# A fused convolution-attention and feed-forward kernel: x loaded one pair later, weight sums one step later, half a layer norm earlier

## The chip, the cores and the metric

The kernel runs on one core of one Trainium2 chip. A core has five engines that work beside each other and meet at semaphores: TensorE (PE in the profile; its weight loads are PEld), VectorE (DVE), ScalarE (ACT), GpSimd (POOL), and SyncE (SP), which here only issues transfers. Transfers are issued from the SP, ACT and POOL queues and are carried by the core's 16 DMA engines. The metric is the device time of one execution in microseconds, as the median of several runs.

## The reference, cut to what matters

Eight images of 32 x 32 positions with 384 channels go through two layers. The first is an attention over all 1024 positions with six heads and relative position terms; the second is a causal attention with one head of 384, and, for the images whose quantization group exists, a feed-forward part with sign weights. There are five groups of one image each, so images 0 to 4 have the feed-forward part and images 5 to 7 don't (their rows of it are zero).

```python
# layer 0
x = x + attention_6_heads(group_norm(x), rel_pos_h, rel_pos_w)  # softmax(q k + rel_h + rel_w) v, then proj
# layer 1
t = tokens(x)
t = t + causal_attention(layer_norm(t), Wq, Wk, Wv)             # softmax(mask(q k / sqrt(384))) v
n = layer_norm(t)                                               # "the second norm" below
h = gelu(quantize(n @ sign(W1 - mean_group(W1)).T + b1))
t = t + quantize(h @ sign(W2 - mean_group(W2)).T + b2)
```

`mean_group` is a mean over a fifth of the output features of the weight matrix; `quantize` scales an image to 8 bits by its largest absolute value.

## The kernel before

Images are worked on one after the other. In layer 0 the six heads are three pairs; a pair's scores come in six bursts (`BURSTS`, 16 units of one block of keys and one half of the queries), and the value products of a burst follow behind the scores of the next. Each unit's exponentials are written into a page of a ring of 12 pages of [128, 1024], and VectorE adds them up (`sums`), which frees the page. The relative position terms of a pair are made in pages of the same ring (`far0`, `far1`, `near`), written to DRAM and read back in another order, split by `place` into a high and a low part, and brought to their places (`r`) by 16 transfers, half of them issued by SP and half by GpSimd.

```python
            def place(p, near, pages):
                for d in range(2):
                    hi, lo, src = (...)
                    nc.scalar.copy(hi, src)                                              # L497
                    nc.vector.tensor_tensor(lo, src, hi.bitcast(F32), ALU.subtract)      # L498
                    if d == 0:
                        yield
                for part in range(4):
                    for d in range(2):
                        for i in range(2):
                            half = part % 2 if d else part // 2
                            (nc.gpsimd if i else nc.sync).dma_start(out=r[part]...,      # L505
                                                                    in_=pages[i]...)
...
            def residual():
                xt = load_x(pools, b)                        # four transfers of 384 KB, issued by SP
                for j in range(NJ):
                    nc.gpsimd.tensor_tensor(xt[:, j, :], xt[:, j, :], pb, ALU.add)       # L551
                return xt
```

The loop over pairs and bursts:

```python
            for p in range(NPAIR):
                sums = [...]
                for n, burst in enumerate(bursts):
                    prs = [scores(p, *u) for u in burst]              # PE L568, L572; ACT L578
                    if b == 0 and (p, n) == (0, 1):
                        multiply_out(pools)                           # wqk: PE L286, evicted by DVE L287
                    for u in pending:
                        values(*u)                                    # DVE L586 (sums), PE L589
                    if n == 0:
                        if p > 0:
                            few = set_aside(p - 1, *last)             # ACT L608, DVE L612, L613
                        elif b > 0:
                            xt = residual()
                        avs = [...]
                    if b == 0 and xt is None and next(signs[0]):
                        xt = residual()
                    if p == 0:
                        with tc.issue_after(last_exp[0]):
                            next(later, None)                         # place() of pairs 1 and 2
                    if n == 2 and p > 0:
                        divide(p - 1, few)                            # PE L621, DVE L597 to L625
                    pending = [...]
```

In image 0 a generator runs beside this: it loads W1 and W2 in three pieces, sums them by group (`w` pieces), forms the means, loads them again (`sign` pieces), makes signs and stores them in DRAM.

```python
        for which, w, _, n_out, _ in pieces("w"):            # the load is issued in pieces()
            for g in range(NG):
                nc.vector.tensor_reduce(part[...], w[:, :, ts(g, n_out // NG)], AX.XY, ALU.add)   # L234
            times[which] += 1
            if which == 1 or w.shape[1] > 1:
                yield False
        ...                                                  # all-reduce of the sums, means
        for which, w, dst, n_out, last in pieces("sign"):
            ...                                              # above = w > m; w = sign (L256, L257)
                    if done > 600:
                        done = 0
                        yield False
            ...
            if last:
                yield True
```

Layer 1's attention goes over eight blocks of keys, its value products two blocks behind, and the feed-forward part begins with the second norm, in two halves of four row blocks each:

```python
            for c in range(NJ):
                prs.append(scores(c))                        # PE L793, DVE L798, ACT L800
                next(other, None)
                for work in signs:
                    next(work, None)
                if c >= 2:
                    values(c - 2)                            # PE L806, DVE L807 to L809
            ...
            values(NJ - 2)
            values(NJ - 1)
...
        def ffn(xt, b, gn):
            xs = [...]
            for half in range(2):
                rs = layer_norm_T(xt, xs[0], half, f"2_{b}", xs[1])
                if half == 0 and gn is not None and pools.fast:
                    with tc.issue_after(last_transpose[0]):
                        ahead[b + 1, 0] = project_qk(b + 1, gn, 0)            # PE L422
```

`layer_norm_T` takes the statistics of four row blocks (DVE L343, L344), a root (ACT L347), and then for each block writes the normalized rows to `xn`, a pool of three buffers (DVE L360), transposes them (PE L298), copies the result rounded (ACT L353) and subtracts to get the rest (DVE L354).

Of the kernel before, what the change touches and what calls it, by code (L numbers as in the profile page):

```python
# [73 lines left out]
def conv_attn_hybrid(  # L74
# [142 lines left out]
    def binarize(pools):  # L217

        def pieces(name):
            for n, piece in enumerate(PIECES):
                room, at = pools.flat(f"{name}_{n}"), 0
                for i, (which, src, sign, k0, k1, n_out) in enumerate(piece):
                    w = room[:, at : at + (k1 - k0) * n_out].rearrange("p (k o) -> p k o", o=n_out)
                    at += (k1 - k0) * n_out
                    nc.gpsimd.dma_start(out=w, in_=src.rearrange("(k p) o -> p k o", p=P)[:, k0:k1, :])
                    yield which, w, sign[:, k0 * n_out : k1 * n_out], n_out, i + 1 == len(piece)

        part = const.tile([P, 2, 2, NG], F32, name="sums_w")  # L230
        times = [0, 0]
        for which, w, _, n_out, _ in pieces("w"):
            for g in range(NG):
                nc.vector.tensor_reduce(  # L234
                    part[:, times[which], which, g : g + 1], w[:, :, ts(g, n_out // NG)], AX.XY, ALU.add
# [53 lines left out]
    def stages(pools):  # L289
# [266 lines left out]
        def attend0_fast(residual, b, q, k, r, v, later):  # L556
# [91 lines left out]
            for p in range(NPAIR):  # L648
                sums = [pools.page(f"sum0_{b}_{p}_{half}") for half in range(2)]
                for n, burst in enumerate(bursts):  # L650
# [5 lines left out]
                    if n == 0:  # L656
                        if p > 0:
                            few = set_aside(p - 1, *last)
                        elif b > 0:
                            xt = residual()  # L660
                        avs = [pools.o_tile(f"av0_{b}_{p}_{half}") for half in range(2)]
                    if b == 0 and xt is None and next(signs[0]):
                        xt = residual()
                    if p == 0:
                        with tc.issue_after(last_exp[0]):
# [73 lines left out]
            return xt, lambda j: None  # L739


        def attention1(xt, more, b, between):
            xT, q = pools.halves(f"lnT_1_{b}"), pools.halves(f"q1_{b}")
            v = pools.flat(f"v1_{b}").rearrange("p (j c) -> p j c", j=NJ)
            nc.gpsimd.memset(v[:, :, C:], 1.0)
# [28 lines left out]

            room = between()
            got = next(room, None)
            (attend1_fast if pools.fast else attend1_general)(xt, b, q, xT, v, room)
            return got

        def attend1_fast(xt, b, q, xT, v, other):  # L780

            room = [pools.flat(f"pr1_{b}_{i}") for i in range(2)]
            tot = pools.small.tile([P, NJ], F32, tag="tot1", name=f"tot1_{b}")
# [30 lines left out]
            for c in range(NJ):  # L814
                prs.append(scores(c))
                next(other, None)
                for work in signs:
                    next(work, None)
                if c >= 2:
                    values(c - 2)  # L820
            for work in signs:
                assert next(work, None) is None
            signs.clear()
            values(NJ - 2)
            values(NJ - 1)
            check(tot, rt, b * (NPAIR + 1) + NPAIR)

        def attend1_general(xt, b, q, xT, v, other):
            next(other, None)
            mask = pools.work.tile([P, P], F32, tag="mask", name=f"mask_{b}")  # L830
            make_causal_mask(nc, mask, mask_val=MASKED)
# [52 lines left out]
            return w1k, w2m  # L884

        def ffn(xt, b, gn):
            xs = [pools.halves(f"{n}_{b}", F32R) for n in ("lnT_2", "lnlo_2")]
            for half in range(2):
                rs = layer_norm_T(xt, xs[0], half, f"2_{b}", xs[1])

                if half == 0 and gn is not None and pools.fast:
                    with tc.issue_after(last_transpose[0]):
                        ahead[b + 1, 0] = project_qk(b + 1, gn, 0)
# [68 lines left out]
                for j in range(NJ):  # L962
                    nc.vector.scalar_tensor_tensor(xt[:, j, :], y[:, j, :], s, xt[:, j, :], ALU.mult, ALU.add)

            return add

        signs = []
        unfinished = []
# [1 line left out]
        def run(pools):  # L970
# [7 lines left out]
            for b in range(B):  # L978
# [4 lines left out]
                    if b + 1 < B:  # L983
                        yield from group_norm_T(b + 1)

                gn = attention1(xt, more, b, between)
                add = ffn(xt, b, gn) if b < B_FFN else None

                def finish(b=b, xt=xt, add=add):
                    if add:  # L990
# [59 lines left out]
```

## Time and profile before

| what | before |
|---|---|
| median of 3 runs | 2481.92 us (2478.55 to 2483.06) |
| span of the profiled execution | 2479.7 us |
| image 0 to 4, one each (layer 0, layer 1, feed-forward) | about 331 us |
| image 5 to 7, one each (no feed-forward) | about 260 us |
| VectorE busy | 1418.0 us (57%) |
| ScalarE busy | 1032.1 us (42%) |
| GpSimd busy | 287.1 us (12%) |
| TensorE's granted clock, mean of the run | 0.99 |

A line of the timeline reads: start and length in us (of a merged group of equal instructions), engine, line of the kernel, operation, output and input tiles, shape, count; in brackets the idle time of the engine ahead of it and the instruction that ended it. A line of the waits reads: engine and its waiting operation, the releaser, and then the total in us, the number of times and the longest. All line numbers are those of the kernel before.

### The profile page before, as it was taken

What the parts mean: (1) busy time and instruction counts of PE and PEld (TensorE: products, weight loads), DVE (VectorE), ACT (ScalarE), POOL (GpSimd) and SP (SyncE); (2) the same over time, 40 slices, a digit from 0 to 9 for tenths busy, and PEclk for the clock granted to TensorE, in tenths of its full rate; (3) what the DMA queues carried; (4) which work ended last, traced back from release to release, by engine and by line L of the source; (5) the groups of instructions that cost most, each with busy time, mean ns of one, the idle gap of its engine ahead of it and who ended that gap; (6) DMA issues with size and microseconds to landing.
All of it is one profiled execution on the core that took longest, in us unless ns stands there. A gap on an engine that the chain in (4) does not pass through costs nothing.

```text
span 2479.7 us, 25709 instructions
## 1 busy us (share of the span) xinstructions
PE 2407.4 (97%) x9378; PEld 1285.8 (52%) x9378; DVE 1418.0 (57%) x2182; ACT 1032.1 (42%) x1756; POOL 287.1 (12%) x389
## 2 busy tenths in 40 slices
PE   7899999999999999999999999999999999999998
PEld 3335585345764456743558534567445443554344
DVE  4596554963466744657545487346674357524752
ACT  3351373532555423645127353256542245124520
POOL 1220002300014000040000230001400030003100
PEclk9899999999999999999999999999999999999999
DMA  7622207211055101181110721004500260018000
GB/s 163 217 77 102 77 1 167 62 64 38 1 102 128 52 13 39 26 184 46 39 39 1 160 70 64 17 22 91 139 26 0 79 149 28 0 47 161 22 1 27
DMA packets 154792, 169.97 MB, mean 69 GB/s; under 512 B 113408, under 2 KB 126048, under 8 KB 153120
## 3 DMA queue, kind: packets, MB, share of 16 engines
q1 hardware_dynamic: 134416, 98.93, 16.9%
q0 software_dynamic: 17184, 69.22, 9.4%
q8 instruction: 77, 1.26, 0.2%
q10 hardware_dynamic: 3056, 0.08, 0.1%
q14 instruction: 59, 0.48, 0.1%
HBM read 75.38 MB, written 42.47 MB: 48 GB/s over the span
## 4 chain that ended last, share of the span: by engine, by line
PE 89%; POOL 4%; DVE 2%; DMA 2%; issue 1%; ACT 1%; SPq 0%; ACTq 0%; DVEq 0%; POOLq 0%
PE f_s L568 12%; PE f_av L589 11%; PE f_qk L422 10%; PE f_s L793 8%; PE f_av L806 8%; PE f_y L949 7%; PE f_y L908 7%; PE f_v L370 5%; PE f_v L517 5%; PE f_q L750 5%; POOL f_x L551 3%; PE f_s L572 3%; PE f_pj L370 2%; PE f_rel L467 2%; PE f_pj L680 2%
## 5 line engine op out<-in xcount | busy, mean ns | idle before, releaser
L578 ACT ACTIVATE f_pr<-f_s 128x512 f32<-128x512 f32 x768 | 408.1, 598 | 377.7 <-PE f_s L572 296.6
L568 PE MATMUL f_s<-f_q,f_k 64*128 64x512 f32 x1536 | 422.4, 616 | 20.3 <-DVE wqk L287 11.0
L589 PE MATMUL f_av<-f_pr,f_v 128*64 128x512 f32 x1536 | 368.7, 608 | 16.3 <-ACT f_pr L578 16.3
L586 DVE TENSOR_TENSOR f_sum<-f_sum,f_pr 128x1024 f32<-128x1024 f32 x288 | 368.3, 1329 | 17.2 <-ACT f_pr L578 16.9
L572 PE MATMUL f_s<-f_r,unit 64*128 64x512 f32 x768 | 312.2, 777 | 0.0
L422 PE MATMUL f_qk<-f_gnT,wqkv_sb 128*128 128x512 f32 x576 | 262.1, 609 | 1.6 <-DVE f_gnT L333 1.6
L568 PEld LDWEIGHTS f_s<-f_q,f_k 64*128 64x128 f32 x1536 | 148.4, 188 | 195.8 <-issue 106.7
L589 PEld LDWEIGHTS f_av<-f_pr,f_v 128*64 128x64 f32 x1536 | 99.6, 137 | 241.5 <-issue 196.4
L793 PE MATMUL f_s<-f_q,f_lnT 128*128 128x512 f32 (+3 forms) x576 | 195.9, 488 | 0.0
L806 PE MATMUL f_av<-f_v,f_pr 128*128 128x385 f32 x576 | 194.5, 486 | 0.0
L422 PEld LDWEIGHTS f_qk<-f_gnT,wqkv_sb 128*128 128x128 f32 x576 | 109.4, 194 | 144.9 <-issue 136.2
L800 ACT ACTIVATE f_pr<-f_s 128x512 f32<-128x512 f32 (+3 forms) x96 | 47.1, 491 | 262.3 <-DVE f_s L798 213.6
L806 PEld LDWEIGHTS f_av<-f_v,f_pr 128*128 128x128 f32 x576 | 108.6, 190 | 78.6 <-issue 11.5
L505 POOL DMA_DIRECT2D f_r<-f_far x192 | 102.2, 534 | 390.4 <-DVE f_far L498 348.1
L793 PEld LDWEIGHTS f_s<-f_q,f_lnT 128*128 128x128 f32 x576 | 102.0, 190 | 77.8 <-issue 54.0
L912 ACT ACTIVATE f_h<-f_y,b_sb 128x256 f32<-128x256 f32 x240 | 100.9, 472 | 68.4 <-PE f_y L908 68.4
L572 PEld LDWEIGHTS f_s<-f_r,unit 64*128 64x128 f32 x768 | 80.8, 189 | 90.9 <-issue 89.0
L750 PE MATMUL f_q<-f_lnT,wqk 128*128 128x512 f32 x288 | 127.5, 592 | 0.0
L919 DVE TENSOR_REDUCE am<-f_h 128x1 f32<-128x1024 f32 (+2 forms) x80 | 71.5, 946 | 97.3 <-ACT f_h L912 97.3
L370 PE MATMUL f_v<-wv_sb,f_lnT 128*128 128x384 f32 x384 | 126.5, 486 | 0.0
L517 PE MATMUL f_v<-wqkv_sb,f_gnT 128*128 128x384 f32 x384 | 125.2, 486 | 0.0
L551 POOL TENSOR_TENSOR f_x<-f_x,pb 128x384 f32<-128x384 f32 x64 | 107.2, 1705 | 18.4 <-DMA f_x<-in_x 18.1
(162 smaller groups left out, 2997.7 us busy)
## 6 DMA issues: line engine op xcount, KB each, us to landing
f_far<-f_far SPq DMA_DIRECT2D x48, 512.0 KB, 3.4
f_r<-f_far POOLq DMA_DIRECT2D x192, 128.0 KB, 3.0
f_r<-f_far SPq DMA_DIRECT2D x192, 128.0 KB, 2.8
f_gnT<-in_xT SPq DMA_DIRECT2D x24, 512.0 KB, 4.6
f_x<-in_x SPq DMA_DIRECT2D x32, 384.0 KB, 6.1
out_y<-f_x POOLq DMA_DIRECT2D x28, 384.0 KB, 4.4
f_near<-f_far SPq DMA_DIRECT2D x128, 64.0 KB, 4.3
f_w1a<-w1s POOLq DMA_DIRECT2D x5, 1536.0 KB, 6.8
```

Source lines behind the costliest of these rows:

```text
L370: nc.tensor.matmul(ps[:, :C], xT[:, k, ts(j, P)], w[:, k, cols], start=(k == 0), stop=(k == NC - 1))
L422: nc.tensor.matmul(made[half], wqkv_sb[:, i, ts(m, P)], xT[:, i, ts(half, 512)], start=(i == 0), stop=(i == NC - 1))
L517: nc.tensor.matmul(ps, keys[:, i, j // 2, j % 2], wqkv_sb[:, i, 2 * C :], start=(i == 0), stop=(i == NC - 1))
L551: nc.gpsimd.tensor_tensor(xt[:, j, :], xt[:, j, :], pb, ALU.add)
L568: nc.tensor.matmul(sc[par], k[rows[par], p, ts(c, P)], q[rows[par], p, ts(half, 512)], start=True, stop=False)
L572: nc.tensor.matmul(sc[par], unit[rows[par], c // 2 % 2].rearrange("i h w -> i (h w)"), r[2 * (c // 4) + c % 2][rows[par], p, ts(half, 512) ...
L578: last_exp[0] = nc.scalar.activation(pr[:, ts(par, 512)], sc[par], AF.Exp).ins
L586: nc.vector.tensor_tensor(sums[half], prev, pr, ALU.add)
L589: nc.tensor.matmul(avs[half][ts(par, HD), :], v[:, c, ts(h, HD)], pr[:, ts(par, 512)], start=(c == 0), stop=(c == NJ - 1),)
L750: nc.tensor.matmul(ps, wqk[:, k, ts(m, P)], xT[:, half, k, :], start=(k == 0), stop=(k == NC - 1))
L793: nc.tensor.matmul(sc[:, lo:], xT[:, c // 4, k, ts(c % 4, P)], q[:, half, k, lo:], start=(k == 0), stop=(k == NC - 1),)
L806: nc.tensor.matmul(av[:, : C + 1], prs[c][:, ts(j - c, P)], v[:, c, :], start=(c == 0), stop=(c == j))
```

## The change

Three things are moved; no operation is added or removed.

The load of x and the adds of pb to it come in the second burst of pair 1 instead of the first burst of pair 0 (images 1 to 7; in image 0 they still follow the first signs). They are only needed at the end of layer 0, and GpSimd also issues transfers of the position terms in pair 0.

The sums of a weight piece come one step of the generator after its load, so that VectorE doesn't stand waiting for the load. The generator has four steps more for it; so that it still ends within layer 1 of image 0, two steps are made there for each block of keys.

The first half of the second norm is put ahead of the last two value products of layer 1, so that PE has those products to do behind its transposes.

```diff
@@ binarize
         for which, w, _, n_out, _ in pieces("w"):
+            yield False
             for g in range(NG):
                 nc.vector.tensor_reduce(
@@ loop over pairs and bursts
                         if p > 0:
                             few = set_aside(p - 1, *last)
-                        elif b > 0:
-                            xt = residual()
                         avs = [pools.o_tile(f"av0_{b}_{p}_{half}") for half in range(2)]
-                    if b == 0 and xt is None and next(signs[0]):
+                    if b == 0 and xt is None and next(signs[0]) or b > 0 and (p, n) == (1, 1):
                         xt = residual()
@@ attend1_fast
                 next(other, None)
-                for work in signs:
+                for work in 2 * signs:
                     next(work, None)
                 if c >= 2:
                     values(c - 2)
             ...
             signs.clear()
+            start()
             values(NJ - 2)
             values(NJ - 1)
@@ ffn
                 rs = layer_norm_T(xt, xs[0], half, f"2_{b}", xs[1])
 
+                if half == 0:
+                    yield
                 if half == 0 and gn is not None and pools.fast:
@@ run
-                gn = attention1(xt, more, b, between)
-                add = ffn(xt, b, gn) if b < B_FFN else None
+                started = []
+
+                def start(gn):
+
+                    if b < B_FFN and not started:
+                        started.append(ffn(xt, b, gn))
+                        next(started[0])
+
+                gn = attention1(xt, more, b, between, start)
+                start(gn)
+                add = next(started[0]) if started else None
```

More of the change, by code (lines that the diff above doesn't have):

```diff
@@ L739, in attend0_general, with attention1 @@
             return xt, lambda j: None
-        def attention1(xt, more, b, between):
+        def attention1(xt, more, b, between, start):
             xT, q = pools.halves(f"lnT_1_{b}"), pools.halves(f"q1_{b}")
@@ L776, in attention1, with attend1_fast @@
             got = next(room, None)
-            (attend1_fast if pools.fast else attend1_general)(xt, b, q, xT, v, room)
+            (attend1_fast if pools.fast else attend1_general)(xt, b, q, xT, v, room, lambda: start(got))
             return got
-        def attend1_fast(xt, b, q, xT, v, other):
+        def attend1_fast(xt, b, q, xT, v, other, start):
             room = [pools.flat(f"pr1_{b}_{i}") for i in range(2)]
@@ L826, in attend1_fast, with attend1_general @@
             check(tot, rt, b * (NPAIR + 1) + NPAIR)
-        def attend1_general(xt, b, q, xT, v, other):
+        def attend1_general(xt, b, q, xT, v, other, start):
             next(other, None)
@@ L963, in add @@
                     nc.vector.scalar_tensor_tensor(xt[:, j, :], y[:, j, :], s, xt[:, j, :], ALU.mult, ALU.add)
-            return add
+            yield add
         signs = []
```

## The prediction

> **What bounds the kernel now.** I read the page's busy table first, then the list of waits of TensorE (PE), then the timeline around each of its waits.
>
> ```profile
> PE 2407.4 (97%) x9378; PEld 1285.8 (52%) x9378; DVE 1418.0 (57%) x2182; ACT 1032.1 (42%) x1756; POOL 287.1 (12%) x389
> ```
>
> TensorE is the bound: 2407.4 of 2479.7 us. No product is added or removed by the change, so it can win only the 72 us in which PE stands idle, and what products lose where they run slowly after a wait. The waits (engine, line, releaser: us in total, times, longest) say where:
>
> ```profile
> PE f_av L589 <- ACT f_pr L578: 16.3, 6, 2.8
> PE f_pt L298 <- DVE xn L360: 12.7, 13, 2.1
> PE f_gmean L320 <- DVE gmv L317: 11.3, 1, 11.3
> PE f_s L568 <- DVE wqk L287: 11.0, 1, 11.0
> PE f_s L568 <- ACT f_pr L578: 9.2, 16, 2.5
> ```
>
> The gmean wait is the first norm of image 0, which the change leaves alone. The other four are what its three parts aim at. First the wait of 11.0, in image 0 (start, length, engine, line; in brackets the idle time ahead and its releaser):
>
> ```profile
> 83.28 1.30 POOL L227 DMA_DIRECT2D f_w<-in_w1T  x2
> ...
> 94.07 4.35 DVE L234 TENSOR_REDUCE sums_w<-f_w 128x1 f32<-128x614 f32 x7 [9.15 <-DMA f_w<-in_w1T]
> 98.34 0.55 DVE L287 TENSOR_SCALAR wqk<-f_wqk 128x384 f32<-128x384 f32 x1
> ...
> 98.94 1.22 PE L568 MATMUL f_s<-f_q,f_k 64*128 64x512 f32 x1 [11.05 <-DVE wqk L287]
> ...
> 105.32 4.96 PE L589 MATMUL f_av<-f_pr,f_v 128*64 128x512 f32 x12
> ```
>
> VectorE (DVE) waits for the loaded weights, and behind it stand the three evictions of wqk, whose PSUM banks the next scores need. Then the wait in pair 0 of image 1, which images 1 to 5 and 7 repeat:
>
> ```profile
> 440.86 11.16 POOL L551 TENSOR_TENSOR f_x<-f_x,pb 128x384 f32<-128x384 f32 x6
> ...
> 451.96 3.18 POOL L505 DMA_DIRECT2D f_r<-f_far  x6
> ...
> 455.29 3.04 ACT L578 ACTIVATE f_pr<-f_s 128x512 f32<-128x512 f32 x6 [8.92 <-DMA f_r<-f_far]
> ...
> 455.94 1.56 PE L589 MATMUL f_av<-f_pr,f_v 128*64 128x512 f32 x4 [2.67 <-ACT f_pr L578]
> ```
>
> GpSimd (POOL) adds pb to x, and its transfers of pair 1's terms queue behind. They read pages of the ring that the exponentials write to, so ScalarE stands 8.92 us and PE 2.67. Last, the second norm (image 2; five images have it):
>
> ```profile
> 955.96 1.15 PE L298 MATMUL f_pt<-ident,xn 128*128 128x128 f32 x9
> ...
> 957.16 1.48 DVE L354 TENSOR_TENSOR f_lnlo<-f_pt,f_lnT 128x384 fp32r<-128x384 f32 x3
> 958.55 0.47 DVE L360 TENSOR_SCALAR xn<-f_x,lmv,lrs 128x384 f32<-128x384 f32 x1
> ...
> 959.17 0.52 PE L298 MATMUL f_pt<-ident,xn 128*128 128x128 f32 x3 [2.06 <-DVE xn L360]
> 959.52 7.01 PE L422 MATMUL f_qk<-f_gnT,wqkv_sb 128*128 128x512 f32 x12
> ```
>
> The statistics and three xn are made long before (from 924.9). The pool of xn has three buffers; the fourth xn waits for transposes and stands behind three subtractions on DVE. That, not the lateness of the norm, is the 2.06 us.
>
> [...] wqk's evictions wait out the 9.15 us of a load that they don't use. [...] six sums beside the adds take 10.93 us, 1.82 each, against 1.23 elsewhere; the adds run from 0.98 to 1.99 us. In image 6 one sum is held for 9.49 us while eight adds run at 0.97. [...] The granted clock is 0.50 from 95 to 106 us; and the twelve qk products after the 2.06 us wait take 6.7 to 7.0 us in images 1 to 3, about 5.2 in images 0 and 4.
>
> **Part 1, x at pair 1 (images 1 to 7).** In the built order the adds now stand behind all sixteen transfers of pairs 1 and 2 and the memset of v1, none among them. The pages of pair 1 are then free about 3 us after the last subtraction of its terms (436.3), near 442, while the stalled exponential was due at 446.4. So that wait goes. Worth per image: 2.67 idle, and four f_av in 1.56 us instead of 0.97 (half of x8 in 1.94), 0.6 us: 3.3. Six images: 20. Image 6: 2.49 idle, and f_av x12 in 4.57 instead of 2.79, 1.8, and slow scores, about 0.7: 5. Sum 25. Remaining in pair 0 are two waits of 0.45 at its start.
>
> The adds still run, some 8 x 1.9 = 15 us. Nothing but the queue holds them: the last terms (DVE L498, 454.26 now) come near 450 once the sums are not slowed, so the adds start near 454, when pair 1 starts, and slow the last three sums of pair 0 by 0.7 each. Transposes (2.36) and `few` (2.3) then end near 465; PE asks for them (L621) near 470. Image 0 now has its adds at 143 to 156, within pair 1, and PE shows no wait there. [...] I take 12% off: 22 us.
>
> **Part 2, sums a step behind (image 0).** The extra yields put the second load (f_w_1, 1536 KB) a step later, and its ten sums behind all three evictions. But in the built order the first five sums still stand ahead of the evictions. So DVE still waits for f_w_0, issued at 83.28. It took 10.8 us to land with 1536 KB of f_w_1 issued within 2.4 us beside it; a load of this size takes 7.7 where the next is issued behind it and 6.8 alone. I take 7 to 8: landing near 91, five sums at 0.65 (3.2), eviction near 94 instead of 98.34. The other two evictions follow at once (0.55 each) instead of among eight sums at 0.4, so the scores that now trickle from 98.94 to 105.3 are done in some 3 us. The next burst of scores, at 110.2 now, starts near 101 to 102: gain 9 us. Against it: f_w_1 lands near 97 and holds the softmax sums to about 99.5; and the ten signs of sign_0, loaded only after the means, stand in one block of 10 x (0.33 + 0.49) = 8 us ahead of pair 1's sums, so pages run short by perhaps a unit: 1 us. Net 8.
>
> **Part 3, second norm ahead (images 0 to 4).** The twelve transposes move ahead of thirty passes of the last value products (9.75 us). In the built order DVE has after value product 5: its three evictions, three subtractions, then the fourth xn. From PE's nine transposes to that xn it is the same chain: value product 5 ends at 946.24, subtractions from 947.45, xn near 948.9, PE resumes near 949.4. The wait of 2.06 moves; it doesn't go. The second half was covered with some 4 us to spare by the qk products; now it has the path product 7, sum, statistics, table load (1.28), root, xn: about 5 us against 5.15 of qk, and its fourth xn may cost 0.4. The three slow qk runs (1.75 each, 5.2 in all) may or may not recur after the moved gap. Net -1 to 0 us; I take 0 to -1.
>
> Sum: 22 + 8 - 1 = 29 us. 2481.9 - 29 = 2453.
>
> **Rivals.** (a) *The adds hurt at their new place.* For: VectorE has more to do in pair 1 than in pair 0 (set aside and divide, about 8 us)[...]. Against: image 0. It would cost 2 to 3 us an image: about 2470. (b) *The norm's wait vanishes*, if the fourth xn comes sooner than the queue says, and the clock stays full: 5 x 2.06 + 5.2 = 15 us more: about 2439. Against it is the position of that xn. (c) *The load lands as late as before*, since sixteen transfers of terms (128 KB each) share the DMA engines (0.90 to 1.02 busy from 84 to 95): then only the trickle is won, 4 us: 2457. (d) *Signs ahead stall image 0* in layer 1, where two steps of signs per row, some 4.5 us, meet rows of 5 us on PE: 2 to 4 us lost.
>
> **Range and chances.** (b) bounds it from below, (a) with (c) and (d) from above: 2439 to 2466 holds it 8 times in 10. Two per cent would be 49.6 us: all of the named waits but gmean (49 us), plus slow clocks, and part 3 keeps its share, so faster by over 2% has 0.02. Slower by over 2% needs a new wait of 11 us in every image: 0.01.
>
> **What would show it.** Right: the wait of f_av on f_pr falls from 16.3 to under 3, none on transfers of f_r; f_s on wqk falls from 11.0 to 5 to 7, f_pt on xn stays at 10 to 13. Wrong: a wait of f_den L621 or of exponentials on f_sum in pair 1; f_s on wqk near 0 or 11; f_pt near 2.

## The result and the profile after

The changed kernel takes 2452.5 us (median of 4 runs, 2450.6 to 2459.4) against 2482.3 us before (4 runs, 2478.6 to 2483.1): a ratio of 0.9888, 95% interval 0.9866 to 0.9910, or 30 us. The prediction was 2453. The profile below is of the run of 2459.4 us; a second profile of the same kernel, of a run of 2451.2 us, comes with the experiments and explains the difference.

The busy table of the changed kernel (engine, busy us, share of the span, instructions):

```profile
PE 2400.5 (98%) x9378; PEld 1286.1 (52%) x9378; DVE 1393.6 (57%) x2182; ACT 1032.6 (42%) x1756; POOL 275.2 (11%) x389
```

The same 9378 products, 6.9 us less busy than before: some of what was won is products that no longer run slowly. Now TensorE's waits (engine, tile and line, releaser: us in all, times, longest). The change shifts most line numbers by one.

```profile
PE f_pt L299 <- DVE xn L361: 12.4, 13, 2.0
PE f_gmean L321 <- DVE gmv L318: 11.3, 1, 11.3
PE f_s L569 <- DVE wqk L288: 10.6, 1, 10.6
PE f_s L569 <- ACT f_pr L579: 6.7, 15, 0.5
PE f_s L569 <- DVE seen L412: 4.0, 1, 4.0
```

Of the four waits that the change aims at, one is gone whole (f_av on f_pr, 16.3 us, six times) and one has lost its long case (f_s on f_pr: 9.2 to 6.7, longest 0.5). The other two stand: 11.0 has become 10.6, 12.7 has become 12.4. And there is a new one: scores that wait for VectorE to read the denominators (`seen`), 4.0 us.

Stage by stage, from the timelines of the two kernels (us; layer 0 is counted from its first score to the first query product of layer 1; layer 1 from there to the first product of the feed-forward part, which in images 0 to 4 includes the second norm):

| stage | before | after | gained |
|---|---|---|---|
| layer 0, image 0 | 144.67 | 150.67 | -6.0 |
| layer 0, images 1, 2, 3 | 124.91, 124.92, 125.01 | 121.55, 121.52, 121.58 | 3.4 each |
| layer 0, images 4, 5, 7 | 126.71, 126.50, 126.65 | 121.54, 121.52, 121.53 | 5.2, 5.0, 5.1 |
| layer 0, image 6 | 127.73 | 121.61 | 6.1 |
| layer 1 and second norm, images 0 to 4 | 89.49, 91.18, 91.18, 91.19, 89.49 | 91.11, 91.12, 91.12, 91.11, 91.12 | -3.1 in all |
| start, to the first score | 70.96 | 72.13 | -1.2 |

Images 1 to 7 give 31.6 us in layer 0, and image 0 and the second norm give part of it back. The start isn't touched by any of the three parts; over all the profiles here it lies between 70.96 and 73.80 us. (Image 0 is longer than the 331 us of images 1 to 4: 349 us before, from its first score to that of image 1.)

**Part 1, image 1.** Timeline around the end of pair 0 (start, length, engine and line; in brackets the idle time ahead and its releaser), GpSimd and VectorE:

```profile
458.68 2.10 POOL L506 DMA_DIRECT2D f_r<-f_far  x4 [6.67 <-DVE f_far L499]
...
460.84 3.87 POOL L552 TENSOR_TENSOR f_x<-f_x,pb 128x384 f32<-128x384 f32 x4
...
465.21 6.31 POOL L552 TENSOR_TENSOR f_x<-f_x,pb 128x384 f32<-128x384 f32 x4 [0.50 <-DMA f_x<-in_x]
...
469.61 2.36 DVE L613 STREAM_TRANSPOSE f_tr<-f_sum 128x1024 f32<-128x1024 f32 x2
471.90 2.30 DVE L614 TENSOR_REDUCE few<-f_tr 128x32 f32<-128x1024 f32 x2
...
478.39 0.26 PE L622 MATMUL f_den<-few,fold 128*64 128x32 f32 x4
```

The adds stand behind the last transfers of terms and end at 471.5. `few` is done at 474.2, and PE asks for it at 478.39 without a wait: 4 us to spare. The adds cost nothing here.

**Part 2, image 0.** Timeline around the first load of weights, in the changed kernel:

```profile
84.44 0.75 POOL L227 DMA_DIRECT2D f_w<-in_w1T  x1
...
95.58 3.59 DVE L235 TENSOR_REDUCE sums_w<-f_w 128x1 f32<-128x614 f32 x5 [9.46 <-DMA f_w<-in_w1T]
99.08 1.48 DVE L288 TENSOR_SCALAR wqk<-f_wqk 128x384 f32<-128x384 f32 x3
...
99.69 1.22 PE L569 MATMUL f_s<-f_q,f_k 64*128 64x512 f32 x1 [10.62 <-DVE wqk L288]
...
104.25 4.94 PE L590 MATMUL f_av<-f_pr,f_v 128*64 128x512 f32 x12
```

The load still lands 11.1 us after its issue, although the second one is now issued 4.6 us later. The three evictions follow each other, so the trickle of scores takes 4.6 us (99.69 to 104.25) instead of 6.4. That is all that is won here. The price comes in pair 1 of the same image:

```profile
135.99 0.67 DVE L257 TENSOR_SCALAR above<-f_sign,mean_w 128x307 f32<-128x307 f32 x2 [3.56 <-DMA f_sign<-in_w1T]
...
138.34 18.02 POOL L552 TENSOR_TENSOR f_x<-f_x,pb 128x384 f32<-128x384 f32 x8 [10.08 <-issue]
...
143.38 2.02 DVE L587 TENSOR_TENSOR f_sum<-f_pr,f_pr 128x1024 f32<-128x1024 f32 x1
...
145.50 2.06 ACT L579 ACTIVATE f_pr<-f_s 128x512 f32<-128x512 f32 x4 [4.64 <-DVE f_sum L587]
...
149.46 0.12 DVE L412 TENSOR_REDUCE seen<-f_den 128x1 f32<-128x32 f32 x1
...
149.73 1.19 PE L569 MATMUL f_s<-f_q,f_k 64*128 64x512 f32 x1 [3.95 <-DVE seen L412]
...
152.13 4.89 PE L590 MATMUL f_av<-f_pr,f_v 128*64 128x512 f32 x12
```

The same place in the kernel before (VectorE and GpSimd):

```profile
140.23 2.35 DVE L586 TENSOR_TENSOR f_sum<-f_pr,f_pr 128x1024 f32<-128x1024 f32 x2
142.50 1.22 DVE L586 TENSOR_TENSOR f_sum<-f_sum,f_pr 128x1024 f32<-128x1024 f32 x1
143.36 13.29 POOL L551 TENSOR_TENSOR f_x<-f_x,pb 128x384 f32<-128x384 f32 x8 [18.15 <-DMA f_x<-in_x]
...
143.96 0.13 DVE L411 TENSOR_REDUCE seen<-f_den 128x1 f32<-128x32 f32 x1
```

Before, the weights of the signs were issued at 99.28, the signs were done by 135.8, among the sums of pair 0, and three sums of pair 1 were made by 143.7. Now GpSimd issues these weights at 127.36, behind the all-reduce for the means, and the ten signs stand in one block (135.99 to 143.4) ahead of pair 1's first sums; those sums take 2.0 us each beside the adds instead of 1.2; the denominators are read after the third of them. Scores that want the PSUM bank (the buffer that the denominators are read from) wait 3.95 us, and then twelve f_av take 4.89 us instead of 2.79. From one product of denominators to the next, pair 1 takes 41.6 us; before it took 33.4. An estimate from these durations: without the adds the three sums would take 3.5 us instead of 5.9, so about 2.4 of the 3.95 us are the adds' and the rest comes from the late start behind the signs.

**Part 3, image 2.** Timeline of the moved norm:

```profile
947.58 1.15 PE L299 MATMUL f_pt<-ident,xn 128*128 128x128 f32 x9
...
950.10 0.47 DVE L361 TENSOR_SCALAR xn<-f_x,lmv,lrs 128x384 f32<-128x384 f32 x1
...
950.72 0.52 PE L299 MATMUL f_pt<-ident,xn 128*128 128x128 f32 x3 [1.99 <-DVE xn L361]
...
951.08 11.57 PE L805 MATMUL f_av<-f_v,f_pr 128*128 128x385 f32 x30
```

The wait has moved with its transposes, and the thirty passes behind it take 11.57 us. The clock granted to TensorE is 0.50 from 951.69 to 955.10 and 1.00 ahead of and behind that.

### The profile page after: what moved, and what is told of

The parts are those of the page before. It is cut to its first block, busy times and chain, and to the rows that moved or that the text cites. A ratio compares the mean times of both kernels' runs of the same rounds, so it can differ in the third digit from the quotient of the medians.

```text
span 2457.7 us, 25707 instructions
## 1 busy us (share of the span) xinstructions
PE 2400.5 (98%) x9378; PEld 1286.1 (52%) x9378; DVE 1393.6 (57%) x2182; ACT 1032.6 (42%) x1756; POOL 275.2 (11%) x389
## 4 chain that ended last, share of the span: by engine, by line
PE 95%; DVE 2%; DMA 1%; ACT 1%; issue 0%; POOL 0%; DVEq 0%; ACTq 0%
PE f_s L569 14%; PE f_av L590 14%; PE f_qk L423 10%; PE f_av L805 8%; PE f_s L792 8%; PE f_y L952 7%; PE f_y L911 7%; PE f_v L371 5%; PE f_v L518 5%; PE f_q L749 5%; PE f_s L573 4%; PE f_pj L371 2%; PE f_rel L468 2%; PE f_pj L679 2%; PE f_pt L299 1%; PE f_pj L684 1%
## 5 line engine op out<-in xcount | busy, mean ns | idle before, releaser
L569 PE MATMUL f_s<-f_q,f_k 64*128 64x512 f32 x1536 | 417.8, 611 | 21.3 <-DVE wqk L288 10.6
L587 DVE TENSOR_TENSOR f_sum<-f_sum,f_pr 128x1024 f32<-128x1024 f32 x288 | 353.8, 1279 | 17.6 <-ACT f_pr L579 17.4
L569 PEld LDWEIGHTS f_s<-f_q,f_k 64*128 64x128 f32 x1536 | 147.2, 186 | 193.5 <-issue 110.6
L805 PE MATMUL f_av<-f_v,f_pr 128*128 128x385 f32 x576 | 203.8, 503 | 0.0
L806 DVE COPY tot<-f_av 128x1 f32<-128x1 f32 x64 | 10.0, 157 | 166.5 <-PE f_av L805 166.5
```

Source lines behind the costliest of these rows:

```text
L569: nc.tensor.matmul(sc[par], k[rows[par], p, ts(c, P)], q[rows[par], p, ts(half, 512)], start=True, stop=False)
L587: nc.vector.tensor_tensor(sums[half], prev, pr, ALU.add)
L805: nc.tensor.matmul(av[:, : C + 1], prs[c][:, ts(j - c, P)], v[:, c, :], start=(c == 0), stop=(c == j))
```

## The experiments

All versions at a glance; the columns of the middle are read from the one profile of each (pair 1 of image 0 between the two products of denominators; how many of the five images run slowly behind the second norm's wait of 2 us, told by 91.1 to 91.2 instead of 89.4 to 89.5 us for layer 1 with the norm).

| version | median us | ratio, 95% interval | pair 1, image 0 | slow of 5 |
|---|---|---|---|---|
| before | 2482 | | 33.4 | 3 |
| part 1 alone | 2452.5 | 0.9884 (0.9867 to 0.9900) | 33.4 | 1 |
| part 2 alone | 2485.2 | 1.0015 (1.0009 to 1.0022) | 38.8 | 4 |
| part 3 alone | 2477.8 | 0.9986 (0.9979 to 0.9993) | 33.4 | 3 |
| parts 1 and 3 | 2453.3 | 0.9882 (0.9865 to 0.9898) | 33.4 | 5 |
| all three: the changed kernel | 2452.5 | 0.9888 (0.9866 to 0.9910) | 41.6 | 5 |
| the changed kernel again | 2451.7 | 0.9875 (0.9859 to 0.9892) | 38.7 | 2 |
| changed, x of image 0 at pair 2 | 2453.3 | 0.9883 (0.9866 to 0.9899) | 38.6 | 5 |
| changed, loads one step later | 2456.2 | 0.9898 (0.9875 to 0.9921) | 40.3 | 4 |
| changed, signs behind sums | 2453.7 | 0.9879 (0.9863 to 0.9896) | 38.1 | 5 |
| changed, wqk on ScalarE | 2460.0 | 0.9915 (0.9899 to 0.9932) | 47.3 | 5 |
| changed, xn in pages | 2437.2 | 0.9817 (0.9800 to 0.9833) | 49.1 | no wait |
| part 1, xn in pages | 2435.9 | 0.9815 (0.9799 to 0.9832) | 33.4 | no wait |
| part 1, xn in pages, loads early | 2422.7 | 0.9761 (0.9744 to 0.9777) | 38.0 | no wait |

### Part 1 alone

```diff
 # the kernel before
-                        elif b > 0:
-                            xt = residual()
...
-                    if b == 0 and xt is None and next(signs[0]):
+                    if b == 0 and xt is None and next(signs[0]) or b > 0 and (p, n) == (1, 1):
                         xt = residual()
```

> The kernel before with part 1 alone: x loaded and its adds made at the second step of pair 1 (images 1 to 7). Theory A, from the stage table of the changed kernel (layer 0 from its first score to layer 1's first query is 3.4 us shorter in images 1 to 3 and 5.0 to 6.1 in images 4 to 7, 31.6 in all): the whole of the gain is part 1, and more than the 29.8 measured, since parts 2 and 3 give some of it back. Then 2450 to 2452 here, and 124.9 to 127.7 us of layer 0 become 121.5 in every image. Theory B, the prediction's own sizes (22 us for part 1, 8 for part 2, -1 for part 3): 2460, and part 2 is needed for the rest. Image 0 should be as it was before: its pair 1 of 33.4 us, wqk wait of 11.0.

2452.5 us: theory A. Layer 0 of images 1 to 7 takes 121.5 to 121.6 us, as in the changed kernel. Waits of TensorE in this version:

```profile
PE f_pt L298 <- DVE xn L360: 12.8, 13, 2.1
PE f_s L568 <- DVE wqk L287: 11.4, 1, 11.4
...
PE f_s L568 <- ACT f_pr L578: 6.7, 15, 0.5
```

Only what part 1 aims at is gone; wqk and xn wait as before. This one part gives all that the three together give, as far as four runs of each can tell.

### Part 2 alone, part 3 alone, parts 1 and 3

```diff
 # part 2 alone
         for which, w, _, n_out, _ in pieces("w"):
+            yield False
             for g in range(NG):
...
-                for work in signs:
+                for work in 2 * signs:
                     next(work, None)
 # part 3 alone: start() ahead of values(NJ - 2), and the yields in ffn that it needs, as in the change
```

> The kernel before with part 2 alone: one more step between each load of weights and its sums, and two steps of signs per row of layer 1. Theory A: the load of the first weights takes its 11 us as before, so only the trickle of scores behind the three evictions is won (6.4 to 4.6 us), and the signs that now come as one block in pair 1 of image 0, beside the adds to x, cost what pair 1 shows (41.6 us against 33.4): 2479 to 2488, no gain. Theory B, the prediction: the load lands 3 us sooner and the evictions follow at once, 8 us net: 2474. Theory C: pair 1's long time in the one profile of the changed kernel was chance, and the rest gives 2 us: 2480. The wait of the scores on wqk: about 10.6 under A and C, 5 to 7 under B.

> The kernel before with part 3 alone: the first half of the second norm ahead of layer 1's last two value products. Theory A: the fourth xn stands where it stood, the wait of 2.0 us moves with the transposes and stays, and TensorE's clock falls after it in all five images instead of three: 2 times 1.7 us lost, 2482 to 2486; wait of f_pt on xn 12 to 13. Theory B: nothing is lost by the move, 2481 to 2482. Theory C, the aim of the part: the wait is covered by the value products, 2467 to 2470; wait of f_pt on xn near 2.

> The changed kernel without part 2 (loads, sums and signs as before). Part 1 alone gave 2452.5, part 3 alone -3.8, part 2 alone +3.6, all three 2452.5. Theory A, the parts add up: 2449, and image 0's pair 1 takes its 33.4 us again. Theory B: part 3's -3.8 was won only where part 1's stall stands (layer 0 of images 4 to 7 took 1.5 to 2.9 us less in that profile[...]), so on top of part 1 it gives nothing, or costs what slow clock follows the moved wait of 2.0 us in each of five images (up to 6.6): 2452 to 2459.

Part 2 costs 3.6 us (interval 2.2 to 5.5): theory A. Its wait on wqk is 10.5 us, and pair 1 of image 0 takes 38.8 us, with a wait of 2.7 on `seen`: the stall was not chance.

Part 3 alone came out 3.8 us faster, which none of its theories had. No wait moved with it (f_pt on xn 12.4, f_av on f_pr 16.6), and three of five images ran slowly behind the norm as before. The profile differs where part 1's stall still stands: layer 0 of images 4 and 6 takes 125.06 and 124.80 us instead of 126.71 and 127.73. In the kernel before, the granted clock over the 3.4 us behind that stall is 0.68 in image 4 and 0.50 in image 6; that it stayed higher there in this version is an estimate, from these durations and from the mean granted clock of the two profiled runs (0.992 against 0.990). This is read from one profile of each, where the 3.8 us are of 20 and 39 runs. With part 1 that stall is gone, and so is the gain: parts 1 and 3 take 2453.3 us, not 2449. So theory B holds there; on top of part 1, four runs show no gain of part 3.

### The changed kernel again

> The changed kernel once more, without an edit. Its one profile is of a run of 2459.4 us, and its three other runs took 2450.6 to 2453.6. Theory A: the difference is image 0's pair 1 (41.6 us in that profile, 33.4 without part 2), by how signs and adds to x fall against each other; in a run of 2451 us pair 1 takes 36 us or less. Theory B: pair 1 takes 38 to 42 in every run, and the difference lies in the start (the first norm, the first load) or in the slow clock after the waits.

2451.2 us in the profiled run. Pair 1 takes 38.7 us here, so the stall is in this run too: theory B, for the greater part. The 8 us between the two profiles are 2.9 in pair 1 and 5.1 in three images that don't run slowly behind the norm. The same two lines as above for image 2 (timeline of TensorE, changed kernel again):

```profile
946.20 0.52 PE L299 MATMUL f_pt<-ident,xn 128*128 128x128 f32 x3 [1.99 <-DVE xn L361]
946.55 9.88 PE L805 MATMUL f_av<-f_v,f_pr 128*128 128x385 f32 x30
```

The same program, the same wait of 1.99 us, and thirty passes in 9.88 us here, 11.57 there. In the first profile the granted clock is 0.50 over the 3.41 us from 951.69 to 955.10. Half the clock for 3.41 us costs 1.7 us, which is the slow stretch (11.57 less 9.88). That the clock stayed full behind this wait here is an estimate, from the 9.88 us and from the mean granted clock of the two profiled runs (0.993 here, 0.990 there).

The same wait differs within one trace too. The norm's wait of 2.06 us in the kernel before is followed by a stretch of 3.41 us at 0.50 in images 1 to 3, and by a clock of 1.00 over the next 3.4 us in images 0 and 4; in the first profile of the changed kernel all five waits of 1.99 to 2.00 us are followed by 3.41 us at 0.50. The stalls of pair 0 in the kernel before, of 2.5 to 2.8 us, are followed by 1.00 over the next 3.4 us in images 1 to 3, and by half the clock in images 4, 5 and 7 (3.41 us each) and in image 6 (6.83 us). So the program sets the wait, and what it costs on top differs from image to image and from run to run; what decides it was not shown.

### Where the 2 us of the second norm come from

```diff
 # layer_norm_T; xlo is given for the second norm only
-                xn = pools.xn.tile([P, C], F32, tag="xn", name=f"xn_{name}_{j}")
+                if xlo is None:
+                    xn = pools.xn.tile([P, C], F32, tag="xn", name=f"xn_{name}_{j}")
+                else:
+                    xn = pools.page(f"xn_{name}_{j}")[:, :C]
```

> The changed kernel with the second norm's xn taken from the twelve page buffers, which are idle then, and not from the pool of three. The fourth xn then has a buffer without waiting for a transpose, and in the built order stands ahead of the evictions. Theory A: the buffer is the cause of the wait of 2.0 us and of the slow clock after it. Then the wait of f_pt on xn goes from 12.4 to under 3, layer 1 with the second norm from 91.1 to 87.4 us in images 0 to 4, and the time is 18 us below the changed kernel: 2434. Theory B: only the wait goes, the clock falls anyway: 5 times 2.0, 2442. Theory C: the xn come late for another reason (statistics, root): no gain, 2452.

> Part 1 alone, and the second norm's xn from the page buffers. Theory A: the buffer of the fourth xn is the whole of the 2.06 us wait, where the norm stands doesn't matter, and image 0 keeps its pair 1 of 33.4 us: layer 1 with the second norm takes 87.4 us in images 0 to 4 as it did with the norm ahead; 2452.5 minus 5 times 2.06, minus 1.7 for the one image that ran slowly after it: 2440, or 2433 if the stall of image 0 (10 us in the profile of the version with part 2) is in every run of that version. Theory B: without part 3 the transposes still wait, since the statistics end too late: 2450.

Waits of the changed kernel with xn in pages:

```profile
PE f_s L572 <- DVE seen L415: 11.7, 1, 11.7
...
PE f_s L572 <- DVE wqk L288: 9.9, 1, 9.9
...
PE f_pt L299 <- DVE xn L364: 2.5, 8, 0.3
```

Theory A: with a buffer for the fourth xn the wait is gone (what is left, 2.5 us, is eight waits of at most 0.3), and so is the slow stretch behind it: layer 1 with the norm takes 87.1 us in every image. On top of part 1 alone, with the norm where it was, it takes 87.3 us. So the buffer was the whole of the wait, and the place of the norm nearly none of it. The median gained 16.6 us on part 1 alone, where the two profiles differ by 12.2: five waits of 2.06, and one slow stretch of 1.7 us. The profiled run of part 1 alone is the fastest of its four (2447.2 us, the median 2452.5); an estimate is that the median run has three slow stretches more. In the profiled run of the changed kernel with pages, image 0 lost 15.7 us in pair 1 (49.1 instead of 33.4, `seen` 11.7); that run took 2443.6 us, the three others 2435.5 to 2437.7, and how much of the loss those have, no profile shows. Part 1 with pages also scatters less: its four runs lie between 2435.0 and 2437.3 us, those of part 1 alone between 2447.2 and 2454.7.

### Where the wait on wqk comes from

```diff
 # changed kernel, wqk on ScalarE
-            nc.vector.tensor_scalar_mul(wqk[:, m, :], ps[:, :C], C**-0.5)
+            nc.scalar.mul(wqk[:, m, :], ps[:, :C], C**-0.5)
```

> The changed kernel with the three evictions of wqk on ScalarE in place of VectorE. They no longer stand behind the sums that wait for the first load. Theory A: that place in VectorE's queue is the wait of 10.6 us: it goes, the three evictions are done near 92 us, image 0 gains 8 to 10 us: 2443. Theory B: the pages run out instead, since VectorE's softmax sums still stand behind the sums of both loads (to 100 us): the wait turns into one of scores or exponentials on f_sum, and 2 to 4 us are won: 2449.

Timeline, changed kernel with wqk on ScalarE:

```profile
84.14 1.43 ACT L288 ACTIVATE wqk<-f_wqk 128x384 f32<-128x384 f32 x3
...
106.62 2.35 DVE L587 TENSOR_TENSOR f_sum<-f_pr,f_pr 128x1024 f32<-128x1024 f32 x2
107.94 1.09 ACT L579 ACTIVATE f_pr<-f_s 128x512 f32<-128x512 f32 x2 [6.25 <-DVE f_sum L587]
108.58 2.07 PE L569 MATMUL f_s<-f_q,f_k 64*128 64x512 f32 x3 [5.38 <-ACT f_pr L579]
```

The evictions are done at 85.6, and the wait on them is gone; the pages then run out, because the softmax sums still stand on VectorE behind the weight sums, and scores wait 5.38 us for an exponential that waits for a sum. Theory B in kind. Pair 1 of image 0 now takes 47.3 us with 10.0 on `seen`: the signs, at their usual 1.5 us for two, hold the first sum of pair 1 to 143.91, when TensorE has already waited for 3.6 us (from 140.28). So here the block of signs makes a stall without the help of the adds. The time is 2460.0, 7.5 us above the changed kernel. Its one profile doesn't show the whole of that: layer 0 of image 0 takes 150.8 us, against 150.7 and 148.0 in the two profiles of the changed kernel, and five images run slowly behind the norm, against five and two. VectorE's queue is the resource here; moving one user out of it let the next one wait.

### Why the load takes 11 us, and who fills pair 1

```diff
 # loads one step later
-                    if b == 0 and xt is None and next(signs[0]) or ...
+                    if b == 0 and xt is None and (p, n) > (0, 0) and next(signs[0]) or ...
 # x of image 0 at pair 2
+                    if b == 0 and not ready and next(signs[0]):
+                        ready.append((p, n))
+                    if (p, n) == ((2, 1) if b == 0 else (1, 1)):
                         xt = residual()
 # signs behind sums: last_sum[0] is the softmax sum that VectorE was given last
+                with tc.issue_after(last_sum[0]):
+                    return next(signs[0])
```

> The changed kernel with the steps of sums and signs begun one step later in image 0, so that the first load of weights is issued after pair 0's first five units instead of the first two. Theory A: the load takes 11 us from issue to landing because sixteen transfers of position terms (128 KB each) share the DMA engines with it; issued later it takes 7 to 8. Theory B: it takes 11 us again, by its own size. In the built order four of its five sums still stand ahead of the first eviction of wqk, so the wait of the scores on wqk stays or grows with the later issue: 2452 to 2458.

> The changed kernel with image 0's x loaded at pair 2, so that its eight adds on GpSimd no longer run beside the ten signs in pair 1. Theory A: the adds and the signs hold each other up (a block of signs took 7.4 us in one profile, 13.3 in another, where the ten should take 8), and without the adds pair 1 of image 0 takes 35 us or less instead of 41.6 to 49: 2446 to 2449, and the runs scatter less. Theory B: the block of ten signs ahead of pair 1's sums is enough by itself: pair 1 takes 38 to 41 us still, 2452.

> The changed kernel, with every step of sums and signs in layer 0 of image 0 held behind the softmax sum that VectorE made last. In the built order the ten signs then stand in blocks of two between pair 1's softmax sums, one block of two ahead of them, and not all ten ahead. The adds to x stay beside them. Theory A: the block of ten ahead of pair 1's sums is the cause of the stall there (38.7 to 41.6 us against 33.4); in blocks of two it goes, pair 1 takes 34 us or less, the wait of the scores on VectorE's reading of the denominators is under 1 us, and the time is 5 us below the changed kernel: 2447. Theory B: signs, adds and sums together are too much for VectorE in pair 1, wherever they stand: pair 1 takes 37 us or more still, 2451.

The first two missed their purpose, because what the program places later the scheduler may still issue early where nothing holds it. The first load was issued at 84.01 (84.44 in the changed kernel) and took 12.0 us. The adds of image 0 began at 137.0 us and not in pair 2. So neither tells its theories apart, and their times, 2456.2 and 2453.3, say nothing of them. The first did move the third load (issued at 120.88 instead of 99.85), and with it the means: in its pair 1 VectorE stands 4.98 us waiting for them ahead of the denominators, and scores wait 4.18 us on `seen`, this time with no block of signs ahead of the sums.

The third did move the signs: blocks of two between pair 1's sums. Timeline, changed kernel with signs behind sums:

```profile
142.67 2.15 DVE L257 TENSOR_SCALAR above<-f_sign,mean_w 128x307 f32<-128x307 f32 x2
...
147.39 0.12 DVE L412 TENSOR_REDUCE seen<-f_den 128x1 f32<-128x32 f32 x1
...
147.66 0.67 PE L575 MATMUL f_s<-f_q,f_k 64*128 64x512 f32 x1 [1.91 <-DVE seen L412]
```

Theory B: pair 1 still takes 38.1 us. Two signs beside the adds (which run from 141.96 to 152.4) take 4.5 us here, 142.67 to 147.2, where two take 1.5 elsewhere in the same run, and the reading of the denominators stands behind them.

### A version aimed at all three causes

```diff
 # part 1 and xn in pages, and:
+                if pools.fast and b == 0 and m == 0:
+                    signs.append(binarize(pools, q[:, 0, 0:1]))
+                    next(signs[0])
...
-        for which, w, _, n_out, _ in pieces("w"):
+        loads = pieces("w")
+        loaded = [next(loads) for _ in range(4)]
+        yield False
+        for which, w, _, n_out, _ in itertools.chain(loaded, loads):
...
+                if name == "w" and n == 0:
+                    nc.gpsimd.tensor_copy(room[:, 0:1], behind)   # holds the loads behind the first q
 # and every step of sums and signs in layer 0 behind the last softmax sum, as above
```

> Part 1 and the second norm's xn in pages (2435.9), and in image 0 all four loads of weights issued right after the first query projection, some 55 us earlier, with every step of sums and signs in layer 0 held behind the softmax sum that VectorE made last. In the built order the three evictions of wqk and the first softmax sums then stand ahead of the last weight sums, and the signs stand in three blocks between softmax sums of pair 0. Theory A: the wait of 11 us comes only from the place of the evictions behind sums that wait for a load; without it and without a block of signs ahead of pair 1 image 0 takes about 134 us from its first score to layer 1 instead of 145: 2425 to 2427. Theory B: the early loads hold back the stores and transfers of the position terms, and what is won at the evictions is lost before the first score (71 us now): 2432 to 2437. Theory C: another wait of image 0 takes the place (pages, as when only the evictions moved): 2436 or more.

2422.7 us: theory A at the evictions, and 2.4% below the kernel before. This is the fastest version of the study. Its waits:

```profile
PE f_gmean L326 <- DVE gmv L323: 11.6, 1, 11.6
PE f_s L586 <- ACT f_pr L596: 6.8, 15, 0.5
PE f_pt L304 <- DVE xn L369: 2.5, 8, 0.3
PE f_s L586 <- DVE seen L420: 1.9, 1, 1.9
```

VectorE in pair 0 of image 0 (timeline of this version):

```profile
86.98 1.49 DVE L293 TENSOR_SCALAR wqk<-f_wqk 128x384 f32<-128x384 f32 x3
...
88.50 2.36 DVE L604 TENSOR_TENSOR f_sum<-f_pr,f_pr 128x1024 f32<-128x1024 f32 x2
...
91.91 3.55 DVE L240 TENSOR_REDUCE sums_w<-f_w 128x1 f32<-128x608 f32 x5
```

The evictions wait for nothing but their products, softmax sums come next, and the weight sums run on data that landed long before. Layer 0 of image 0 takes 132.0 us instead of 145.1 in part 1 with pages, nearly the whole of the 13.2 us between the medians: pair 0 is 17.7 us shorter there and pair 1 4.7 longer. Two things were changed at once; signs behind sums alone, on the changed kernel, had given nothing (2453.7). Unlike the version with wqk on ScalarE, this one also frees the softmax sums from the load.

This run also answers what the load needs. Issued near 22.8 us, with 3072 KB of other weights issued within 2 us of it, the load of 1536 KB landed after 8.4 us. At 85.84 another load of the same size (the first signs' weights) took its old place among the transfers of terms, with no other load behind it, and took 11.2. In the changed kernel the third load, of the same size and issued at 99.85, when those transfers are through, took 7.4, and the signs' weights, issued near 127, took 6.9 to 8.6. So it is the company at the start of pair 0 and not the second load that makes the first one slow; which of the transfers there does it isn't shown.

One stall is left in image 0, and it shows what the block of signs had hidden. Timeline, same version, start of pair 1:

```profile
124.24 11.11 POOL L563 TENSOR_TENSOR f_x<-f_x,pb 128x384 f32<-128x384 f32 x8 [6.82 <-issue]
...
127.90 3.25 DVE L604 TENSOR_TENSOR f_sum<-f_pr,f_pr 128x1024 f32<-128x1024 f32 x2
...
133.29 0.12 DVE L420 TENSOR_REDUCE seen<-f_den 128x1 f32<-128x32 f32 x1
...
133.56 0.87 PE L586 MATMUL f_s<-f_q,f_k 64*128 64x512 f32 x1 [1.89 <-DVE seen L420]
```

No sign is left in pair 1 (the last ends at 123.4), and pair 1 still takes 38.0 us. The adds begin at 124.2, four us ahead of the denominators' product at 128.1; pair 1's first sums take 1.6 to 2.0 us each beside them, and the denominators are read after three of them. In the kernel before and with part 1 alone the adds of image 0 begin with that product (143.36 and 143.4; 143.81 and 143.84), when two sums are already made, and nothing waits. In images 1 to 7 of the changed kernel they end 3.7 to 6.9 us ahead of it. So a stall is there with no sign in pair 1. But the adds are not alone to blame: the signs of pair 0 stand ahead of the set-aside, and the first sum begins at 127.90, 0.2 us ahead of the product, where before it began 3.2 us ahead (140.23). An estimate: with sums of 1.2 us each, 0.2 of the 1.89 us would be left. A version that also holds image 0's adds until pair 1's denominators are read was not tried.

## Why the prediction was right, point by point

The total was met: 2453 predicted, 2452.5 measured. Of its three terms one was right, and the errors of the two others nearly cancel (part 1 7 to 10 us too small, part 2 some 12 too large). The mechanism of the largest term was right; that the total came out within 1 us was luck.

**Part 1, 25 us less 12%: mechanism right, undersized by 7 to 10 us.** The waits went, the two of 0.45 us at pair 0's start stayed, and the times at the new place were met. The prediction had adds from 454, `few` at 465 and the question for it at 470 on the old clock; this profile's image 1 begins 8.65 us later (its first score is at 429.07 instead of 420.42), which makes 462.7, 473.7 and 478.7, and the trace has 460.8, 474.2 and 478.4. Two terms of the sum were mis-sized. The 3.3 us per image was read in image 1 and taken times six: images 1 to 3 gained 3.4, but images 4, 5 and 7 gained 5.0 to 5.2, because in the kernel before TensorE's clock fell behind their stalls (granted 0.65 to 0.68 over the next 3.4 us; 1.00 in images 1 to 3), and image 6 gained 6.1 instead of 5. That is 6.6 us more: 31.6. And the 12% for rival (a) was not needed: no add hurt in images 1 to 7.

**Part 2, net 8 us gained: wrong, it costs 3.6.** The step that failed first is the landing of the load, "I take 7 to 8: landing near 91". It took 11.1 us and landed at 95.5, as in rival (c), since what runs beside it at the start of pair 0, and not the second load, slows it. With it fell the eviction at 94 (99.08) and the burst at 101 to 102 (109.1); counted from the first score, 2.3 us were won instead of 9. The second failed step is "pages run short by perhaps a unit: 1 us". Pair 1 of image 0 lost 5.4 to 8.3 us in the two profiles. The block of ten signs was seen, but not that it meets the adds to x in image 0, beside which a sum takes 2.0 us, and that the read of the denominators, and so a PSUM bank, stands behind all of it. Two of the prediction's own signs of being wrong came true here: exponentials that wait for f_sum in pair 1 (4.64 us) and f_s on wqk near 11 (10.6 us). Rival (d) blamed the signs in layer 1; nothing waits for them there.

**Part 3, 0 to -1 us: right.** The wait of 2.06 moved and stayed as 1.99, because of the fourth xn, as worked out from the queue; the runs with pages show the cause. The second half of the norm lost nothing, not even the 0.4 set down for it. The slow stretches of 1.7 us behind the wait, "may or may not recur", are in five images of one profile and two of another.

**Sum.** 22 + 8 - 1 = 29 was the prediction. Part 1 alone gave 29 (interval 25 to 33), and parts 2 and 3 together nothing that can be measured beside it. Part 2's cost of 3.6 us is known from its 20 runs against the kernel before; on top of parts 1 and 3 (2453.3 without it, 2452.5 with it) it is not resolved. The trace of the kernel before already spoke against the first of part 2's steps: the load that took 7.7 us there has 1536 KB issued right behind it, so a load behind it could not be what made the first one take 10.8. And the range, 2439 to 2466, is said to be bounded by rival (a) from above, which alone was put at 2470.

## What to carry to other kernels

In this kernel an operation that waited on an engine's queue was cured where the queue was blocked: giving the next user its own buffer (xn in pages, 15 to 17 us) or making the blocked operand arrive long before (loads early, 13 us) worked, while moving one victim to another engine or moving the wait to another place only chose the next victim. Before a stall is multiplied by the number of places it occurs in, look at each of them, because the stretch of slow products behind the same wait differs from one to the next, and from run to run (here none, or 1.7 us behind a wait of 2 us). And where the program moves work that nothing holds, look at what the scheduler did with it before reading a time: two of the edits here did not move what they were meant to move.

## What the runs showed of the hardware that was not expected

- The same wait of TensorE was followed by half the clock in some images and by full clock in others. Behind the norm's wait of 2.06 us in the kernel before the granted clock was 0.50 for 3.41 us in three images (1.7 us lost each) and 1.00 in two; behind the 1.99 to 2.00 us of the changed kernel it was 0.50 for 3.41 us in all five. The two profiles of the changed kernel differ by three slow stretches (5.1 us).
- The eight adds on GpSimd, in one block, took between 10.4 (signs behind sums) and 18.0 us (changed kernel) in image 0, and beside them a softmax sum took 2.0 us (changed kernel) instead of 1.2. Signs took longer beside them in one version: with the adds at 10.4 us (signs behind sums) two took 4.5 us instead of 1.5, while with the adds at 18.0 us (changed kernel) two kept their 1.5.
- A load of 1536 KB of W1 or W2 took 6.7 to 13.1 us in these kernels. One issued 0.93 us behind another of the same size took 10.6 (kernel before, 99.28); the one ahead of it took 7.7.
